# Graph attention on one core: the last output pair and the single tile turned by VectorE, adds of x and scatters two products later

## The chip, the cores and the metric

One core of one Trainium2 chip. The time is that of one execution on the device in microseconds, lower is better: a median of a few runs, and beside it one profiled execution, which every row of the trace comes from. The engines are TensorE (PE, with its weight loads as PEld), VectorE (DVE), ScalarE (ACT), GpSimd (POOL) and SyncE (SP). DMAs are issued by SP, ACT and POOL, each on a queue of its own.

## The reference

```python
h = jnp.maximum(_layernorm(x, axis=-1), 0.0)           # x: 2708 x 1024, float32
q = h @ W_q.T + b_q
k = h @ W_k.T + b_k
v = h @ W_v.T + b_v
z = (q @ k.T) / sqrt(1024)
z = z * adj                                            # adj: 0 or 1, density 0.0014771
z = jnp.where(z == 0.0, -10000.0, z)
out = x + relu(softmax(z, axis=1) @ v)
```

A row of adj has about four ones. The rest of its row of scores is -10000 and vanishes in the softmax, so a row of the output needs a handful of rows of h and no more.

## The kernel before

The keys' projection is folded into that of the queries (M, formed in the first hundred microseconds), and the values' projection is applied after the sum: a row of the output is relu(u @ W_v + b_v) + x, where u is the weighted sum of the neighbours' rows of h. Rows are sorted by their number of neighbours, so that a tile of 128 sorted rows needs K gathers of 128 rows each. `tab` holds, for each sorted row, its neighbours and its number in x.

Of the sorted tiles, 20 form ten q pairs (units 0 to 9) and 20 form ten o pairs (units 10 to 19); the last o pair is (16, 9), and tile 8 is left alone (`single`). A unit is one product of a 256x1024 block with a 1024x1024 matrix, done by `multiply` as seven smaller products of a 2x2 scheme (Strassen's in Winograd's form), each of four matmuls of 128x512 on one PSUM bank. Its operands a11, a12, a22 and s1 to s4 are formed one unit ahead by `blocks`: `upper` takes both halves of the first tile, `lower` those of the second, and VectorE forms s1 to s4. `between` starts the first two products of the next unit ahead of the last one of this unit, and for tile 8 the first product of the single.

A tile has to be turned for this (its columns on the partitions). There are two ways:

- on PE: `half_turned` issues four transposes of 128x128 into PSUM, and ScalarE copies them out (line 718) or VectorE adds from them. `turned` does both halves of a tile.
- "faced": ScalarE copies the finished sum u into v with its columns rearranged (line 944), stores v to `u_dram` (line 946), SP loads it back by quarters with `by_quarters` (line 700, four DMAs of 128 KB into a tile named or), and `faces` has VectorE transpose blocks of 32x32 (line 705).

`sums` decides which way a tile goes (line 940), by the place (unit and step) at which its sum is complete. `near` keeps a sum in SBUF (`held`) when its unit is close.

The attention runs beside the products as a generator (`attention`: `scores` multiplies gathered rows with q rows, L863; `weights`; `sums`, L923). `advance(share)` lets it run so many estimated microseconds of VectorE at each of the seven steps `after(0)` to `after(6)` of a unit. VectorE's order is the written one; for PE, ScalarE, POOL and SP a scheduler orders the instructions from unit 4 on. All four then run in their fixed order.

The result of an o unit is written into two y tiles (a pool of four buffers); `add_x` gathers rows of x onto it with an adding DMA, and `scatter` writes it to its rows of the output, both from POOL (lines 1109 and 808). `send` places a scatter behind the add of the next tile. For the last pair `ends` gathers the rows of x first and VectorE adds. `tail` handles the last 20 rows.

Of the kernel before, what the change touches and what calls it, by code (L numbers as in the profile page):

```python
# [18 lines left out]
P = 128  # L19
# [46 lines left out]
def tile_preln_masked_attention(  # L66
# [852 lines left out]
    def sums(t):  # L919
        u, coef, m = us.pop(t)  # L920
        for s in range(0 if t in EMPTY else 1, K[t]):
            fill()
            chained(lambda: nc.vector.scalar_tensor_tensor(  # L923
                u, g_of[t][s], coef[:, s:s + 1], u, op0=ALU.mult, op1=ALU.add))
            free.append(g_of[t][s])
            yield 1.3
        fill()
        if t in HOSTS:
            chained(lambda: nc.vector.scalar_tensor_tensor(
                u[:HP], g_of[t][K[t]][:HP], m[:HP, 3:4], u[:HP], op0=ALU.mult, op1=ALU.add))  # L930
            free.append(g_of[t][K[t]])
            yield 1.3
            fill()
        g_of.pop(t)
        if t == SECOND:
            nc.sync.dma_start(v_dram, u)
            whole_second.append(True)
            return
        unit = next((n for n, pair in enumerate(units) if pair[0] == "o" and t in pair[1:]), len(units))
        if now < [unit - 2, 2] and unit <= len(q_pairs) + 4:  # L940
            faced_tiles.add(t)
        if t in faced_tiles:
            v = row_tile(f"v_{t}")
            nc.scalar.copy(v.rearrange("p (a c r) -> p c a r", a=QUADS, r=QP),
                           u.rearrange("p (c a r) -> p c a r", a=QUADS, r=QP))
            nc.scalar.dma_start(u_dram[t * P:(t + 1) * P, :], v)
        elif near(t):
            held[t] = u
        else:
            nc.sync.dma_start(u_dram[t * P:(t + 1) * P, :], u)  # L950
        done.add(t)
# [159 lines left out]
    def o_results(ta, tb):  # L1111
        ya = work.tile([P, D], FT, tag="q", name=f"y_{ta}", bufs=4)
        yb = work.tile([P, D], FT, tag="q", name=f"y_{tb}", bufs=4)
        if (ta, tb) == o_pairs[-1]:
            return ends(ya, ta, yb, tb)

        def c11(X):
            nc.scalar.activation(ya[:, lo], X, AF.Relu)

        def c22(Y, p5):  # L1120
            nc.vector.tensor_add(p5, copied(Y), p5)
            nc.scalar.activation(yb[:, hi], p5, AF.Relu)

        def c12(Z, u2):
            nc.vector.tensor_add(u2, Z, u2)
            nc.scalar.activation(ya[:, hi], u2, AF.Relu)
            if ta == NT - 2:

                nc.sync.dma_start(tail_dram, ya[P - 1:, :])
            send(add_x(ya, ta))  # L1130
            sent.append((ya, ta))

        def c21(Y):
            nc.scalar.activation(yb[:, lo], Y, AF.Relu)  # L1134
            send(add_x(yb, tb))
            sent.append((yb, tb))

        return c11, c22, c12, c21

# [23 lines left out]

        return c11, c22, c12, c21

    sent = []

    def send(behind):

        while sent:  # L1170
            y, t = sent.pop(0)
            with tc.issue_after(behind.ins):
                scatter(y, t, P)

    def tail(t):
        n = tiles[t][1]
        y = work.tile([P, D], FT, tag="q", name=f"y_{t}", bufs=4)
        nc.sync.dma_start(y[:n], tail_dram.to_broadcast([n, D]))
        add_x(y, t, n)
        scatter(y, t, n)  # L1180

    def of_wv(i, j):

# [41 lines left out]
    for n, unit in enumerate(units):  # L1225
# [4 lines left out]
            ordered.enter_context(tc.manual_schedule(engines={mybir.EngineType.DVE}))  # L1230
            nc.sync.dma_start(bp_dram, bp_sb[0:1, :])
        turn = n in (0, FIRST - 1)
        share = 20.9 / 7
        nxt = units[n + 1] if n + 1 < len(units) else None
        if nxt is not None and nxt[0] == "o":
            share -= 2.3 / 7 * len(set(nxt[1:]) & faced_tiles)
# [1 line left out]

        def after(i):
            now[1] = i  # L1240
            if (n, i) in steps_ahead:
                follow(steps_ahead[n, i])
            if (n, i) == (2, 5):
                owe(8)
                owe(9)
                rows_of[FIRST] = load_rows(units[FIRST])
                owe(10)
                owe(6)
                owe(7)
                rows_of[FIRST + 1] = load_rows(units[FIRST + 1])  # L1250
                pooled.close()
            if (n, i) == (FIRST, 1):
                for g in slots[:HIGH - 3]:
                    nc.vector.memset(g, 0.0)
            b11, b12, b21, b22 = M[:, 0, 0], M[:, 0, 1], M[:, 1, 0], M[:, 1, 1]
            for at, place, src in (((-1, 0), b12, of_wv(0, 1)), ((0, 0), b11, of_wv(0, 0)), ((0, 2), T[:, 1], of_wv(1, 1)),
                                   ((0, 3), b21, of_wv(1, 0)), ((0, 4), b22, of_wv(1, 1))):
                if (n - last_q, i) == at:
                    nc.sync.dma_start(place, src)
            for at, place, a, b in (((0, 2), T[:, 0], b12, b11), ((0, 4), T[:, 1], T[:, 1], T[:, 0]),  # L1260
                                    ((1, 0), T[:, 2], b22, b12), ((1, 1), T[:, 3], b21, T[:, 1])):
                if (n - last_q, i) == at:
                    nc.vector.tensor_sub(place, a, b)
            if (n - last_q, i) == (1, 1):
                free.extend(M.rearrange("p i j (a c) w -> p i j a (c w)", a=2)[:, 0, 1, a, :] for a in range(2))
            if (n, i) == (FIRST, 5):
                next(stream)
            if (n, i) == (FIRST, 6):
                chain.append(behind[-1])
                next(stream)  # L1270
                nc.vector.tensor_tensor(bad, bad, total, op=ALU.not_equal)
            if (n, i) == (FIRST + 1, 6):
                marked(EARLY, NT)
            if (n, i) == (FIRST + 2, 4):
                nc.vector.tensor_scalar(msq, msq, MLIMIT, None, op0=ALU.is_gt)
            if n > FIRST + 1 or n == FIRST + 1 and i > 1:
                advance(share)
            if nxt is not None:

                if i == (3 if n == 0 else 4 if turn else 0):  # L1280
                    ops_of[n + 1] = blocks(*rows_of[n + 1], nc.gpsimd if n + 1 < FIRST - 1 else None)
                    with tc.issue_after(products[-1].ins) if n + 1 == FIRST else nullcontext():
                        ops_of[n + 1][1]()
                if i == (4 if n == 0 else 5 if turn else 2):
                    ops_of[n + 1][2]()
                    rows_of.pop(n + 1)
                    if n == last_q - 1:
                        all_rows()
                if i == 3:
                    banks_of[n + 1] = banks_for(bp_sb)  # L1290
                if i == 6 and n + 2 < FIRST:
                    natural_rows(n + 2)
                if i == (2 if n in (FIRST, last_q) else 4) and n + 2 > FIRST and n + 2 < len(units) and n + 2 not in rows_of:
                    while units[n + 2][0] == "o" and not done.issuperset(units[n + 2][1:]):
                        advance(1.0)
                    rows_of[n + 2] = load_rows(units[n + 2])
            if (n, i) in steps_at:
                follow(steps_at[n, i])
            if (n, i) == (3, 4):
                searched()  # L1300
            if (n, i) == (3, 5):
                for s in range(8, HIGH):
                    for c in range(0, D, D // 4):
                        clear = nc.gpsimd.memset(slots[s][:, c:c + D // 4], 0.0)
                        tc.add_manual_dep(clear.ins, counted_at[-1].ins.name,
                                          mybir.DependencyInfo(mybir.DependencyClass.Sync, mybir.DependencyReason.DATA),
                                          reason="not beside the counts")
            if i == 3 and units[n - 1][0] == "o" and NT - 2 in units[n - 1][1:]:
                tail(NT - 1)
            if nxt is None and i == 1:  # L1310
                while alone not in done:
                    advance(1.0)
                r, = load_rows(("o", alone))
                single["turned"] = turned(r, "alone")
            if nxt is None and i == 3:
                single["banks"] = banks_for(bp_sb)
            if n == last_q - 1 and i == 4:

                nc.sync.dma_start(bp_sb, bv.to_broadcast([P, D]))
            if (n, i) == (last_q, 1):  # L1320
                nc.vector.tensor_sub(bp_sb[:, NB:], bp_sb[:, NB:], bp_sb[:, :NB])
# [233 lines left out]
```

## Time and profile before

| | |
|---|---|
| median of three runs | 639.91 us (639.73 to 640.34) |
| the profiled execution | 639.94 us, its span 638.1 us |
| granted PE clock | 0.997 |
| PE busy | 98% of the span |
| VectorE busy | 82% |
| ScalarE, GpSimd busy | 44%, 56% |
| HBM | 292 GB/s over the span |

A row of a timeline gives start, length, engine, line of the kernel, operation, output and inputs with their shapes, and in brackets how long the engine had been idle and what ended that. "u", "or", "pt" and so on are the names of tiles without their numbers. A matmul of float32 shows as two records. The tail behind the last product is part of the span.

### The profile page before, as it was taken

The numbers are of one execution on the slowest core, as the hardware profiler recorded it, in microseconds if no ns is written. First come the engines' busy times: TensorE is split into PE (matmuls) and PEld (weight loads), VectorE is DVE, ScalarE is ACT, GpSimd is POOL, SyncE is SP. The second block draws the span as 40 slices with busy tenths as digits, with TensorE's granted clock in tenths as the row PEclk, the third lists the DMA queues.
The fourth block names the chain that finished last, engine by engine and source line by source line (L and its number), as shares of the span: only waits on it lengthen the run. The fifth ranks groups of instructions, "written<-read, shape, count | busy, mean of one in ns | idle before, by whom it ended". The sixth has DMA issues, their size and how long they took to land.

```text
span 638.1 us, 6156 instructions
## 1 busy us (share of the span) xinstructions
PE 627.8 (98%) x1651; PEld 317.9 (50%) x1651; DVE 522.4 (82%) x1016; ACT 283.6 (44%) x423; POOL 360.2 (56%) x383
## 2 busy tenths in 40 slices
PE   9999999999999999999999999999999999999994
PEld 5777766444444444444444444444444444444441
DVE  5999888997997625999888999999999889989121
ACT  3538985849667533424342144343342432333200
POOL 2639960885768357565651663476466878633311
PEclk9999999999999999999999999999999999999998
DMA  8999997598796439996798998999999999853631
GB/s 335 407 362 321 342 351 286 200 323 330 255 379 231 171 95 317 327 323 223 233 299 289 290 414 222 295 344 311 363 382 325 325 290 291 266 145 77 187 119 50
DMA packets 60192, 176.96 MB, mean 277 GB/s; under 512 B 9799, under 2 KB 15255, under 8 KB 59512
## 3 DMA queue, kind: packets, MB, share of 16 engines
q0 software_dynamic: 25136, 78.41, 39.4%
q1 hardware_dynamic: 29514, 78.61, 35.0%
q10 hardware_dynamic: 5502, 19.48, 7.8%
q8 instruction: 15, 0.25, 0.2%
q14 instruction: 25, 0.20, 0.1%
HBM read 145.65 MB, written 40.74 MB: 292 GB/s over the span
## 4 chain that ended last, share of the span: by engine, by line
PE 90%; issue 4%; POOL 2%; DMA 2%; DVE 1%; POOLq 0%; ACT 0%; ACTq 0%; DVEq 0%
PE ps L1010 40%; PE psy L1010 29%; PE ps_y L476 6%; PE ps_x L476 4%; PE ps_z L476 4%; PE pt L415 4%; POOL g L610 2%; DMA v_dram<-u 1%; DMA M<-h_dram,tab 1%; PE ps_y L511 1%; DVE junk L863 0%; PE ps_h L1218 0%; PE ps_v L594 0%; DVE u L923 0%; DVE s L722 0%
## 5 line engine op out<-in xcount | busy, mean ns | idle before, releaser
L610 POOL DMA_INDIRECT g<-h_dram,tab x94 | 120.2, 1278 | 79.9 <-DVE u L923 30.0
L1010 PE MATMUL psy<-wlow,s 128*128 128x512 f32 x320 | 144.0, 592 | 0.0
L1010 PE MATMUL ps<-M,a 128*128 128x512 f32 x320 | 144.0, 593 | 0.0
L863 DVE SCALAR_TENSOR_TENSOR junk<-g,pq 128x1024 uint8<-128x1024 f32 x93 | 113.8, 1224 | 13.4 <-DMA g<-h_dram,tab 10.4
L1010 PEld LDWEIGHTS ps<-M,a 128*128 128x128 f32 x320 | 59.7, 190 | 70.4 <-issue 69.1
L923 DVE SCALAR_TENSOR_TENSOR u<-g,coef,u 128x1024 f32<-128x1024 f32 x69 | 88.4, 1281 | 7.0 <-ACT u L912 5.8
L1010 PEld LDWEIGHTS psy<-wlow,s 128*128 128x128 f32 x320 | 59.6, 190 | 69.2 <-issue 69.0
L389 DVE FIND_INDEX8 at<-ones,adj 128x8 uint32<-128x685 f32 (+1 forms) x88 | 74.5, 864 | 0.0
L1010 PE MATMUL ps<-wlow,s 128*128 128x512 f32 x160 | 72.0, 593 | 0.4 <-DVE s L722 0.4
L1010 PE MATMUL ps<-M,s 128*128 128x512 f32 x160 | 72.1, 592 | 0.0
L1010 PE MATMUL psy<-wlow,a 128*128 128x512 f32 x160 | 72.0, 593 | 0.0
L368 ACT ACTIVATE sized<-adj 128x2708 uint8<-128x2708 f32 (+1 forms) x22 | 54.3, 2467 | 7.4 <-DMA adj<-in_adj_dram 6.1
L298 POOL TENSOR_TENSOR hsum<-hsum,x 128x256 f32<-128x256 f32 (+1 forms) x56 | 38.6, 732 | 26.2 <-DVE wlow L444 22.5
L1109 POOL DMA_INDIRECT y<-in_x_dram,tab x19 | 34.2, 1798 | 28.9 <-ACT y L1134 12.1
L1010 PEld LDWEIGHTS ps<-wlow,s 128*128 128x128 f32 x160 | 30.3, 190 | 38.9 <-issue 38.5
L1010 PEld LDWEIGHTS psy<-wlow,a 128*128 128x128 f32 x160 | 30.3, 190 | 38.5 <-issue 37.3
L1010 PEld LDWEIGHTS ps<-M,s 128*128 128x128 f32 x160 | 30.3, 190 | 38.1 <-issue 37.4
L808 POOL DMA_INDIRECT out_dram<-y,tab x21 | 27.4, 1306 | 32.0 <-DMA y<-in_x_dram,tab 15.8
L912 ACT ACTIVATE u<-g,coef 128x1024 f32<-128x1024 f32 x18 | 20.7, 1149 | 35.8 <-DVE coef L911 35.6
L276 ACT ACTIVATE x<-x,r 128x1024 f32<-128x1024 f32 (+1 forms) x22 | 25.9, 1232 | 6.6 <-POOL r L266 6.6
L722 DVE TENSOR_TENSOR s<-a,pt 128x512 f32<-128x512 f32 x30 | 19.2, 681 | 10.9 <-ACT a L718 10.9
L476 PE MATMUL ps_y<-wlow 128*128 128x512 f32 x64 | 27.6, 592 | 0.0
(251 smaller groups left out, 843.3 us busy)
## 6 DMA issues: line engine op xcount, KB each, us to landing
adj<-in_adj_dram SPq DMA_DIRECT2D x21, 1354.0 KB, 11.5
x<-in_x_dram SPq DMA_DIRECT2D x21, 512.0 KB, 8.2
h_dram<-x ACTq DMA_DIRECT2D x21, 512.0 KB, 7.4
q_late<-q SPq DMA_DIRECT2D x12, 512.0 KB, 5.1
pq<-q_late SPq DMA_DIRECT2D x12, 512.0 KB, 6.6
u_dram<-v ACTq DMA_DIRECT2D x10, 512.0 KB, 6.4
or<-u_dram SPq DMA_DIRECT2D x40, 128.0 KB, 7.0
M<-in_wv_dram SPq DMA_DIRECT2D x4, 1024.0 KB, 8.4
```

Of the source, the lines that this page charges most:

```text
L276: nc.scalar.activation(xs[i][:n], xs[i][:n], AF.Relu, bias=r[:n, 4, i:i + 1], scale=r[:n, 3, i:i + 1])
L298: small.append(nc.gpsimd.tensor_add(hsum[:n, cols], hsum[:n, cols], xt[:n, cols]))
L368: nc.scalar.activation(sized[:n], a[:n, :, :PW], AF.Abs, accum_out=total[:n, t:t + 1])
L389: nc.vector.max_index(at[:n, k - first_k, g, :], ones[:n, 0:8], a[:n, g, :])
L415: nc.tensor.transpose(pt[:, c, :], xt[:, k * P:(k + 1) * P], ident)
L476: mm = nc.tensor.matmul(bank, a_tile(o + H * a[0], a[1], i), b(o), start=first and o == 0, stop=(o == H - 1), skip_group_check=True)
L610: return nc.gpsimd.indirect_dma_start(out=dst, out_offset=None, in_=src, in_offset=off, bounds_check=N - 1, oob_is_err=False)
L808: to = nc.gpsimd.indirect_dma_start(out=out, out_offset=bass.IndirectOffsetOnAxis(ap=ptab.bitcast(U32)[:n, t, SLOTS:SLOTS + 1], axis=0), i ...
L863: chained(lambda: nc.vector.scalar_tensor_tensor(junk, g_of[t][s], 1.0, tq[t], op0=ALU.mult, op1=ALU.mult, accum_out=zall[:, t, s:s + 1]))
L923: chained(lambda: nc.vector.scalar_tensor_tensor(u, g_of[t][s], coef[:, s:s + 1], u, op0=ALU.mult, op1=ALU.add))
L1010: mm = nc.tensor.matmul(bank, a[:, c, :], b[:, c, :], start=False, stop=(c == 3), skip_group_check=True)
L1109: return nc.gpsimd.indirect_dma_start(out=y[:n], out_offset=None, in_=x, in_offset=off, compute_op=ALU.add)
```

## The change

- The tiles of the last pair (16 and 9) and the single tile 8 are always faced: `or unit >= len(units) - 1`. Tile 8 is loaded at the end of the last unit but one, and turned whole by VectorE at step 1 of the last.
- The add of x for a result is no longer issued where the result is written, but two products later (`due`, `add_due`), and a scatter stays back by one more add (`stay`).
- The tail tile is taken from the pool of rows instead of the pool of y, and its scatter goes through `sent` too.
- The share of VectorE per step grows from 20.9/7 to 21.5/7 in the last five units.

```diff
-        if now < [unit - 2, 2] and unit <= len(q_pairs) + 4:
+        if now < [unit - 2, 2] and unit <= len(q_pairs) + 4 or unit >= len(units) - 1:
             faced_tiles.add(t)
...
-            send(add_x(ya, ta))
-            sent.append((ya, ta))
+            due.append((now[0], 5, ya, ta))
...
             nc.scalar.activation(yb[:, lo], Y, AF.Relu)
-            send(add_x(yb, tb))
-            sent.append((yb, tb))
+            due.append((now[0] + 1, 1, yb, tb))
...
-    sent = []
-    def send(behind):
-        while sent:
-            y, t = sent.pop(0)
+    sent, due = [], []
+    def add_due():
+        while due and due[0][:2] <= tuple(now):
+            y, t = due.pop(0)[2:]
+            send(add_x(y, t), 1)
+            sent.append((y, t, P))
+    def send(behind, stay=0):
+        while len(sent) > stay:
             with tc.issue_after(behind.ins):
-                scatter(y, t, P)
+                scatter(*sent.pop(0))
...
-        y = work.tile([P, D], FT, tag="q", name=f"y_{t}", bufs=4)
+        y = row_tile(f"y_{t}")
         nc.sync.dma_start(y[:n], tail_dram.to_broadcast([n, D]))
         add_x(y, t, n)
-        scatter(y, t, n)
+        sent.insert(0, (y, t, n))
...
-        share = 20.9 / 7
+        share = (20.9 if n < len(units) - 5 else 21.5) / 7
...
         def after(i):
             now[1] = i
+            add_due()
...
             if nxt is None and i == 1:
+                uT = work.tile([P, D], FT, tag="hT", name="T_alone", bufs=2).rearrange("p (c q) -> p c q", q=P)
+                faces(uT, single["rows"], 0, DC)
+                single["turned"] = uT
+            if n == len(units) - 2 and i == 6:
                 while alone not in done:
                     advance(1.0)
-                r, = load_rows(("o", alone))
-                single["turned"] = turned(r, "alone")
+                single["rows"], = load_rows(("o", alone))
```

In the order of the instructions this shows at three places. First PE, from the first two products of the last pair's predecessor to the last pair's own; u_16 and u_9 are the sums of tiles 16 and 9. Before:

```order
L1010 MATMUL ps1_3541<-wlow_171,s1_3520 128x512 x4
L1010 MATMUL psy_3427<-wlow_171,a22_3357 128x512 x4
L415 MATMUL pt_3598<-ident_75,u_16_3416 128x128 x4
L415 MATMUL pt_3605<-ident_75,u_16_3416 128x128 x4
L1010 MATMUL psy_3571<-wlow_171,s2_3524 128x512 x4
L415 MATMUL pt_3633<-ident_75,u_9_3499 128x128 x4
L415 MATMUL pt_3640<-ident_75,u_9_3499 128x128 x4
L1010 MATMUL ps0_3539<-M_148,a12_3464 128x512 x4
```

and after:

```order
L1011 MATMUL ps1_3544<-wlow_171,s1_3526 128x512 x4
L1011 MATMUL psy_3426<-wlow_171,a22_3360 128x512 x4
L1011 MATMUL psy_3588<-wlow_171,s2_3530 128x512 x4
L1011 MATMUL ps0_3542<-M_148,a12_3475 128x512 x4
L1011 MATMUL ps1_3544<-M_148,s4_3532 128x512 x4
```

The four rows of transposes are gone, and the two of u_8 one unit later are gone in the same way. Second VectorE at the end of the program, around the turning of tile 8, which is new there (before, ScalarE copied T_alone out of PSUM). zs and many belong to a sum that decides whether the data need the general path (not taken here), y_16 and p5 to the results of the last pair. After:

```order
L705 STREAM_TRANSPOSE T_alone_3710<-or_8_3698 128x4x8x32
L1145 SCALAR_TENSOR_TENSOR y_16_3703<-ps0_3655,y_16_3703 128x512
L1340 SCALAR_TENSOR_TENSOR zs_3753<-zall_102,keys_93 128x352
L1341 TENSOR_TENSOR zs_3753<-zall_102 128x352
L1342 SCALAR_TENSOR_TENSOR zs_3753<-zs_3753 128x352
L1343 TENSOR_REDUCE many_139<-zs_3753 128x1
L1155 TENSOR_TENSOR u2_3716<-ps1_3657,u2_3716 128x512
L1350 TENSOR_TENSOR many_139<-many_139,deg_98 128x1
L1145 SCALAR_TENSOR_TENSOR y_16_3703<-u2_3716,y_16_3703 128x512
L1352 TENSOR_TENSOR many_139<-many_139,deg_98 128x1
L1151 TENSOR_TENSOR p5_3691<-psy_3685,p5_3691 128x512
```

and before:

```order
L1343 TENSOR_TENSOR many_139<-many_139,deg_98 128x1
L1146 SCALAR_TENSOR_TENSOR y_16_3701<-ps0_3660,y_16_3701 128x512
L1156 TENSOR_TENSOR u2_3723<-ps1_3662,u2_3723 128x512
L1146 SCALAR_TENSOR_TENSOR y_16_3701<-u2_3723,y_16_3701 128x512
L1152 TENSOR_TENSOR p5_3692<-psy_3686,p5_3692 128x512
```

The zs group used to stand ahead of y_16; now it stands behind the turning, and between it and the read of bank psy by p5 there are nine steps. Third POOL, from the add of x for tile 14 on. Before:

```order
L1109 DMA y_14_3590<-in_x_dram,tab_97 128x1024
L808 DMA out_0_dram<-y_10_3447,tab_97 2708x1024
L612 DMA y_16_3701<-in_x_dram,tab_97 128x1024
L612 DMA y_9_3702<-in_x_dram,tab_97 128x1024
L1109 DMA y_1_3591<-in_x_dram,tab_97 128x1024
L808 DMA out_0_dram<-y_14_3590,tab_97 2708x1024
L808 DMA out_0_dram<-y_1_3591,tab_97 2708x1024
L612 DMA y_alone_3780<-in_x_dram,tab_97 128x1024
```

and after:

```order
L1110 DMA y_14_3605<-in_x_dram,tab_97 128x1024
L808 DMA out_0_dram<-y_15_3445,tab_97 2708x1024
L612 DMA y_16_3703<-in_x_dram,tab_97 128x1024
L808 DMA out_0_dram<-y_10_3446,tab_97 2708x1024
L808 DMA out_0_dram<-y_14_3605,tab_97 2708x1024
L1110 DMA y_1_3606<-in_x_dram,tab_97 128x1024
L612 DMA y_9_3704<-in_x_dram,tab_97 128x1024
L612 DMA y_alone_3773<-in_x_dram,tab_97 128x1024
L808 DMA out_0_dram<-y_1_3606,tab_97 2708x1024
```

Each scatter (out_0_dram) has moved behind one more add of x; the gather into y_16 stands right behind the scatter of tile 15, whose buffer it takes.

More of the change, by code (lines that the diff above doesn't have):

```diff
@@ L939, in sums @@
         unit = next((n for n, pair in enumerate(units) if pair[0] == "o" and t in pair[1:]), len(units))
-        if now < [unit - 2, 2] and unit <= len(q_pairs) + 4:
+        if now < [unit - 2, 2] and unit <= len(q_pairs) + 4 or unit >= len(units) - 1:
             faced_tiles.add(t)
+        print("done", t, "at", now, "unit", unit, t in faced_tiles)
         if t in faced_tiles:
```

## The prediction

> **What bounds the kernel now.** I read the page first, then who TensorE (PE) waited for, then the chain that ended last.
>
> ```profile
> span 638.1 us, 6156 instructions
> PE 627.8 (98%) x1651; PEld 317.9 (50%) x1651; DVE 522.4 (82%) x1016; ACT 283.6 (44%) x423; POOL 360.2 (56%) x383
> ```
> ```profile
> PE ps_y L511 <- POOL hsum L121: 1.2, 1, 1.2
> PE ps L1010 <- DVE s L722: 0.4, 1, 0.4
> ```
> PE is busy for 627.8 of 638.1 us. In the whole span it waits twice: 1.2 us at the start and 0.4 us once for VectorE. What is left, 638.1 - 627.8 - 1.6 = 8.7 us, is the tail after its last product. So each microsecond taken from PE's own work shortens the run, as long as nothing that PE reads comes later than PE does. The chain near the end shows what the change takes away:
>
> ```profile
> 571.59 0.88 PE pt L415 x8
> ...
> 575.90 0.88 PE pt L415 x8
> ...
> 597.38 0.87 PE pt L415 x8
> ...
> 629.41 0.70 DVE y_alone L1371
> ```
> The first three are the turnings of tiles 16, 9 and 8. Behind the last product there is one step on VectorE (the last row) and a scatter, which the change does not touch, so that tail stays.
>
> **Removed.** The three groups of eight transposes: 0.88 + 0.88 + 0.87 = 2.63 us of a PE that never pauses there. The measured time of this profiled run was 639.94 us (span and 1.84 around it), 0.03 above the median of 639.91, so the two can be used alike. The floor is 639.94 - 2.63 = 637.31 us. ScalarE also loses five copies out of PSUM; it is busy for 44% of the span, so that is worth nothing by itself.
>
> **Added: a round trip for three tiles.** Each finished sum u is now copied on ScalarE into v, stored to DRAM, loaded back by quarters on SP's queue, and turned on VectorE. For 16 and 9 this ends long before PE needs it. For tile 8, the last, it is close, and that is the whole question. The rows for it, of VectorE and then of ScalarE (start and length in us, engine, line, operation; in brackets the idle time ahead of it and what ended that):
>
> ```profile
> 446.58 1.30 DVE L705 STREAM_TRANSPOSE a<-or 128x512 f32<-128x512 f32 x2
> 408.92 0.71 DVE L705 STREAM_TRANSPOSE a<-or 128x512 f32<-128x512 f32 x1
> 412.99 1.28 DVE L923 SCALAR_TENSOR_TENSOR u<-g,coef,u 128x1024 f32<-128x1024 f32 x1
> 547.51 1.28 DVE L923 SCALAR_TENSOR_TENSOR u<-M,coef,u 128x1024 f32<-128x1024 f32 x1
> 558.72 2.60 DVE L923 SCALAR_TENSOR_TENSOR u<-g,coef,u 128x1024 f32<-128x1024 f32 x2
> 562.38 0.69 DVE L1121 TENSOR_TENSOR p<-taken,p 128x512 f32<-128x512 f32 x1
> 571.74 0.08 DVE L863 DVE_READ_ACCUMULATOR junk<-g,pq 128x1 f32 x1
> 574.59 5.25 DVE L923 SCALAR_TENSOR_TENSOR u<-g,coef,u 128x1024 f32<-128x1024 f32 x4 [1.66 <-ACT u L912]
> 579.75 1.28 DVE L722 TENSOR_TENSOR s<-a,pt 128x512 f32<-128x512 f32 x2
> 582.27 2.60 DVE L923 SCALAR_TENSOR_TENSOR u<-M,coef,u 128x1024 f32<-128x1024 f32 x2
> 586.70 1.28 DVE L929 SCALAR_TENSOR_TENSOR u<-g,m,u 64x1024 f32<-64x1024 f32 x1
> 589.49 0.52 DVE L1331 SCALAR_TENSOR_TENSOR zs<-zall,keys 128x352 f32<-128x352 f32 x1
> ```
> ```profile
> 419.21 1.05 ACT L944 COPY v<-u 128x1024 f32<-128x1024 f32 x1 [0.57 <-DVE u L923]
> 420.29 0.33 ACTq L946 DMA_DIRECT2D u_dram<-v  x1
> 549.38 1.15 ACT L912 ACTIVATE u<-M,coef 128x1024 f32<-128x1024 f32 x1 [1.48 <-DVE coef L911]
> 561.33 0.58 ACT L1075 COPY taken<-psy 128x512 f32<-128x512 f32 x1 [1.85 <-PE psy L1010]
> ```
> *When is u_8 complete?* Before, at 586.70 + 1.28 = 587.98. Both engines work in a fixed order, so each step put ahead delays it:
> - the copy v_16 stands ahead of the first multiple of tile 9 on ScalarE: u_16 is complete at 548.79, the copy ends at 549.84 where that multiple had begun at 549.38: +0.5;
> - the copy v_9 and its store stand ahead of the copy "taken": 561.32 + 0.5 + 1.05 + 0.33 + 0.58 = 563.8, where the add behind it on VectorE would have begun at 562.38 + 0.5: +0.9;
> - two turnings for tile 16: +1.3. For tile 9, two turnings with the four adds behind them took 412.99 - 408.92 = 4.07; the four adds alone, between the rows at 579.75 and 582.27, take 2.52: +1.55;
> - the add of p that stood behind the last sum now stands ahead of it: +0.6;
> - the wait of 1.66 for ScalarE shrinks, since ScalarE has no copies from PSUM ahead of that multiple, and the short wait before it is filled by the turnings: I take -0.7.
>
> Together +4.15: u_8 is complete at 592.1, its copy at 593.2.
>
> *When must T_alone be there?* PE reads it first, and the product right behind is added on a bank that VectorE must have read:
>
> ```profile
> 590.35 3.60 PE L1010 MATMUL ps<-wlow,s 128*128 128x512 f32 x8
> 611.82 3.60 PE L1010 MATMUL ps<-M,T_alone 128*128 128x512 f32 x8
> 615.25 3.60 PE L1010 MATMUL psy<-wlow,a 128*128 128x512 f32 x8
> ```
> PE reaches T_alone at 611.82 - 2.63 = 609.2 and that product at 612.6. But on VectorE, T_alone now stands ahead of everything up to the read of that bank: four operations of the size of the row of 0.69, four of 0.52 and two tiny ones, 5.0 us. So the turning has to end by 612.6 - 5.0 = 607.6, earlier than the 609.2 that PE's own read would allow.
>
> *The trip between.* Store and quarter loads have rows of their own; the first answer is for v, the others for the quarter loads of three stretches (380 to 395, 395 to 405 and 431 to 440 us), and last the stretches as a whole (their last two numbers are the share of DMA time and GB/s):
>
> ```profile
> DMA to landing us min/median/max: 6.1/6.4/6.9
> ```
> ```profile
> L700 SPq DMA_DIRECT2D or<-u_dram x8: 302/394/432, 387.4 to 392.1; - x8
> ...
> DMA to landing us min/median/max: 4.3/5.0/5.5
> ```
> ```profile
> DMA to landing us min/median/max: 8.1/8.4/8.6
> ```
> ```profile
> DMA to landing us min/median/max: 13.1/14.1/15.1
> ```
> ```profile
> 387.00:397.00 10.00, 9.64 (x23) 4.08 (x22) 9.83 (x15) 3.89 (x7) 3.99 (x3) 1.00 0.91 191
> 401.00:412.00 11.00, 11.00 (x27) 4.90 (x26) 10.76 (x21) 4.63 (x8) 5.31 (x5) 1.00 1.06 277
> 600.00:610.00 10.00, 10.00 (x24) 4.37 (x23) 2.00 (x3) 1.17 (x2) 2.93 (x3) 1.00 0.76 209
> ```
> The store lands at 593.2 + 6.4 = 599.6. Four issues of 0.39 follow; the last goes out at about 601.0 and lands L later; the turning takes 1.3. T_alone ends at 602.35 + L, and the loss is S = L - 5.25 where that is positive. L is the term that the trace of before bounds only from afar: 4.3 to 15.1. I take the row of 380 to 395 (5.0; in all 191 GB/s with eight loads), because the stretch 600 to 610 moved 209 GB/s without quarter loads, only four are added, and nothing else stands on SP's queue; the row of 8.4 comes from a stretch with 277 GB/s and gathers every 1.3 us. L from 4.3 to 5.5 gives S from 0 to 0.3; I take 0.1. Sum: 637.31 + 0.1 = **637.4 us**.
>
> Rule against row: the Trainium skill ("DMA: Bandwidth & Descriptors", Anatomy of one DMA) puts a transfer at some 2.0 us plus its bytes at 436 GB/s. An estimate from that page is 2.3 us for a quarter and 3.2 for the store, which would leave S at 0 and the time at 637.31. The rows above disagree: 4.3 is the fastest of that stretch and 6.1 the fastest store.
>
> *Tiles 16 and 9.* The store of v_16 goes out at 551.1, lands at 557.5, its last quarter leaves at about 559.0, and VectorE comes to it at 571.74 + 0.5 + 0.9, 573.2: L up to 14 is hidden. For v_9: out at 562.9, landed 569.3, last quarter 570.8, VectorE at 580.5 (the first sum of tile 8 at 574.59 + 0.5 + 0.9 + 1.3 - 0.7 = 576.6, and three sums of 1.29): L up to 9.7 is hidden. The sums s1 are then ready at 582.6, PE wants them at 590.35 - 1.76 = 588.6.
>
> **Moved, at no cost that I can find.** On POOL's queue each scatter now stands behind one more add of x, and two gathers come ahead of an add that they stood behind. What the old order cost POOL between 410 and 600 us, then the rows of a scatter, of the last gather of h rows, of ScalarE's write into a y buffer, and of a scatter's landing:
>
> ```profile
> POOL out_dram L808 <- DMA y<-in_x_dram,tab: 7.0, 3, 3.2
> ```
> ```profile
> 550.54 1.03 POOL L808 DMA_INDIRECT out_dram<-y,tab  x1 [0.30 <-issue]
> ...
> 556.73 1.01 POOL L610 DMA_INDIRECT g<-h_dram,tab  x1 [0.30 <-issue]
> ```
> ```profile
> 563.10 0.63 ACT L1122 ACTIVATE y<-p 128x512 f32<-128x512 f32 x1 [1.19 <-DVE p L1121]
> ```
> ```profile
> out_dram<-y,tab POOLq DMA_INDIRECT x21, 6.5
> ```
> 7.0 us of POOL waiting goes, worth 0 to at most the 0.4 us that PE waited for VectorE at all, and that was near 389 us, ahead of the first scatter: I take 0. The price would be a y buffer that comes free later: tile 12's scatter leaves at about 550.5 instead of 537, lands 6.5 later at 557, and ScalarE writes the buffer again at 563.10. Six microseconds cover it. The larger budget for the last five units puts one sum (1.28) ahead of the four adds; those are 588.6 - 582.6 = 6 us early at the worst place. The tail tile in another pool and the changed place of its load on SP delay nothing that PE reads.
>
> **Rivals.**
> - *The loads of tile 8 share the DMA engines with the delayed scatters* (those of tiles 10 and 14 now stand behind tile 15's scatter and behind a gather into its buffer, so they fall into the same stretch). For it: the 8.4 row. Then S = 3.15 and 640.5: the gain is used up. From L = 6.5 on (S = 1.25) it is no longer a gain of 0.2%. Chance 0.18 for L between 6.5 and 9.1.
> - *Slower: the same loads wait as the worst did*, 13.1 to 15.1 (the stretch from 431 us). Then S = 7.9 to 9.9 and 645.2 to 647.2. It decides from L = 9.1 (S = 3.9). Against it: in that stretch gathers were queued; the last of them goes out at 556.73. With tile 9's loads beyond 9.7, which push the same step, chance 0.13.
> - *VectorE becomes the bound.* The Trainium skill ("VectorE: DVE Perf Modes", Rules for kernel authors) advises TensorE for turning 128x128. By the rows, eight blocks take 0.88 us on PE and 1.3 on VectorE, so the rule holds engine by engine, but PE is the one that is full. It would decide if the adds for the last pair came 6 us later than worked out; a further 4 us beyond that, and 639.94 - 2.63 + 4 = 641.3. Chance 0.03.
>
> **Chances and range.** Forecast with S below 1.3: 0.66. A measurement of this kernel can tell about 0.2%, 1.28 us, from no change, so faster is below 638.63 and slower above 641.19: faster 0.66, same 0.18, slower 0.16. The range goes down to 636.8 (the floor, less the 0.4 us wait should it vanish, less 0.1) and up to 640.6, which takes in S = 3.3, the row of 8.4.
>
> **What would show it.** Right: no pt rows of 571 to 598 us; the last quarter load of or_8 lands by 606.3, T_alone is turned by 607.6, PE's waits in the last 30 us are under 0.3 us, and the span is 2.5 us shorter. Wrong: a wait of PE at T_alone or at the product after it, with VectorE idle for or_8 ahead of it; a landing of or_8 over 6.5; VectorE waiting for or_16 or or_9; or ScalarE held up by a y buffer.

## The result, and the profile after

| | before | changed |
|---|---|---|
| median | 640.34 us (639.63 to 642.51, 7 runs) | 637.2 us (636.89 to 639.33, 7 runs) |
| ratio | | 0.9961, 95% interval 0.9945 to 0.9976 |
| PE busy in the profiled execution | 627.8 us | 625.4 us |

The change is faster by 0.4%, some 2.5 us of 640 (1.5 to 3.5). The ratio, which comes with the interval, is what is used below; it is not the quotient of the two medians, which would be 0.9951. The profiled execution of the changed kernel was one of its slower ones (639.16 us, span 637.1), so its span must not be set against the 638.1 of before. Its page and the list of whom PE waited for:

```profile
span 637.1 us, 6134 instructions
...
PE 625.4 (98%) x1627; PEld 315.4 (49%) x1627; DVE 524.7 (82%) x1021; ACT 284.8 (45%) x421; POOL 362.7 (57%) x383
```
```profile
PE ps_y L511 <- POOL hsum L121: 1.2, 1, 1.2
PE pt L415 <- DMA qr<-h_dram,tab: 0.7, 1, 0.7
PE ps L1011 <- DVE s L722: 0.6, 1, 0.6
PE ps_in L678 <- DVE sort L666: 0.4, 1, 0.4
```
PE has 2.4 us less to do. It waits 2.9 us in all where it waited 1.6 before, and all four waits lie in the first 391 us, ahead of everything that the change touches. These 1.3 us more of early waiting are why this one execution is only 1.0 us shorter in span. No wait of PE ends behind 391 us.

The rows that answer to those of the prediction, of VectorE, ScalarE and PE (the changed file's lines are one higher here):

```profile
573.63 1.30 DVE L705 STREAM_TRANSPOSE a<-or 128x512 f32<-128x512 f32 x2
...
580.73 0.70 DVE L705 STREAM_TRANSPOSE a<-or 128x512 f32<-128x512 f32 x1
...
591.09 1.27 DVE L929 SCALAR_TENSOR_TENSOR u<-g,m,u 64x1024 f32<-64x1024 f32 x1
604.96 1.25 DVE L705 STREAM_TRANSPOSE T_alone<-or 128x1024 f32<-128x1024 f32 x1 [11.53 <-DMA or<-u_dram]
611.04 0.69 DVE L1151 TENSOR_TENSOR p<-psy,p 128x512 f32<-128x512 f32 x1 [0.89 <-PE psy L1011]
```
```profile
562.22 1.04 ACT L945 COPY v<-u 128x1024 f32<-128x1024 f32 x1 [0.56 <-DVE u L923]
...
592.39 1.05 ACT L945 COPY v<-u 128x1024 f32<-128x1024 f32 x1 [0.56 <-DVE u L929]
593.47 0.33 ACTq L947 DMA_DIRECT2D u_dram<-v  x1
```
```profile
610.84 3.60 PE L1011 MATMUL ps<-M,T_alone 128*128 128x512 f32 x8
614.27 3.60 PE L1011 MATMUL psy<-wlow,a 128*128 128x512 f32 x8
```
The turnings of 16 and 9 have no bracket: VectorE did not wait for their rows. For tile 8 it waited 11.53 us with nothing else to do, turned at 604.96, and its add into p ended at 611.73, after 0.89 us of waiting for PE. The product that must follow that add begins at 614.27. So VectorE could have been 614.27 - 611.73 + 0.89 = 3.4 us later before PE lost anything. I call this the *room* below.

The quarter loads of tiles 16, 9 and 8, by stretch:

```profile
L700 SPq DMA_DIRECT2D or<-u_dram x4: 330/500/1092, 556.6 to 558.0; - x4
...
DMA to landing us min/median/max: 10.4/10.4/10.4
```
```profile
L700 SPq DMA_DIRECT2D or<-u_dram x4: 303/431/505, 571.0 to 572.4; - x4
...
DMA to landing us min/median/max: 3.5/3.5/3.5
```
```profile
L700 SPq DMA_DIRECT2D or<-u_dram x4: 303/430/431, 597.6 to 598.9; - x4
...
DMA to landing us min/median/max: 5.1/5.1/5.1
```
In each of these stretches the view tells the landing of one quarter of the four, which is why its three figures are equal. The same instruction landed in 10.4, 3.5 and 5.1 us. The quarter of the 5.1 is not the last one: from the last issue for tile 8, at 598.9, to the turning at 604.96 there are 6.1 us.

### The profile page after: what moved, and what is told of

It reads as the page before. It is cut to its first block, busy times and chain, and to the rows that moved or that the text cites. A ratio compares the mean times of both kernels' runs of the same rounds, so it can differ in the third digit from the quotient of the medians.

```text
span 637.1 us, 6134 instructions
## 1 busy us (share of the span) xinstructions
PE 625.4 (98%) x1627; PEld 315.4 (49%) x1627; DVE 524.7 (82%) x1021; ACT 284.8 (45%) x421; POOL 362.7 (57%) x383
## 4 chain that ended last, share of the span: by engine, by line
PE 87%; issue 4%; DVE 4%; DMA 2%; POOL 2%; POOLq 0%; ACT 0%; ACTq 0%; DVEq 0%
PE ps L1011 39%; PE psy L1011 27%; PE ps_y L476 6%; PE ps_z L476 4%; PE ps_x L476 4%; PE pt L415 4%; POOL g L610 2%; DMA v_dram<-u 1%; DVE g L1260 1%; DMA M<-h_dram,tab 1%; PE ps_y L511 1%; DVE s L722 0%; DVE at L389 0%; DVE junk L863 0%; PE ps_h L1223 0%
## 5 line engine op out<-in xcount | busy, mean ns | idle before, releaser
L610 POOL DMA_INDIRECT g<-h_dram,tab x94 | 123.7, 1316 | 81.7 <-DVE u L923 33.0
L1110 POOL DMA_INDIRECT y<-in_x_dram,tab x19 | 32.6, 1717 | 29.9 <-ACT y L1127 15.3
L808 POOL DMA_INDIRECT out_dram<-y,tab x21 | 25.7, 1224 | 17.7 <-DVE flag L1355 7.3
L760 ACT COPY ps<-bp_sb 128x512 f32<-128x512 f32 x42 | 24.6, 595 | 6.0 <-DVE y L1145 5.5
```

The lines of the kernel that those rows point to most:

```text
L610: return nc.gpsimd.indirect_dma_start(out=dst, out_offset=None, in_=src, in_offset=off, bounds_check=N - 1, oob_is_err=False)
L808: to = nc.gpsimd.indirect_dma_start(out=out, out_offset=bass.IndirectOffsetOnAxis(ap=ptab.bitcast(U32)[:n, t, SLOTS:SLOTS + 1], axis=0), i ...
L1110: return nc.gpsimd.indirect_dma_start(out=y[:n], out_offset=None, in_=x, in_offset=off, compute_op=ALU.add)
```

## The experiments

The kernel before was timed again in each of the four sets. Its median was 640.17 us in the first (the parts apart) and 640.44 in the third (how late the scatters must be, more tiles), but 647.5 in the second (which part, the room) and 645.9 in the fourth (the flags), where most executions had a granted clock of 0.987 to 0.995. The first and the fourth set ran on the same chip, the second and the third on two others, so the chip alone does not make this difference. Only ratios are compared across sets. "The deferral" below takes in the tail's new tile and the place of its scatter; no run tests that part by itself.

### The parts apart

The theory from the trace: facing three tiles is worth 2.63 us of PE, and the deferral is worth nothing.

*Facing alone*: the condition and the early load of T_alone, with adds, scatters, tail and share as before.

```diff
-        if now < [unit - 2, 2] and unit <= len(q_pairs) + 4:
+        if now < [unit - 2, 2] and unit <= len(q_pairs) + 4 or unit >= len(units) - 1:
```


> Tiles 16, 9 and 8 turned by VectorE, but adds, scatters, tail tile and shares as before. If the gain is PE's transposes alone (theory A): 2.6 us under before, as the changed kernel, ratio 0.996; PE's busy time 2.6 less. If the later adds and scatters carry part of it (theory B, at least 1 us): at most 1.6 under before. If the scatters that now lie earlier clear the DMA engines for the loads of tile 8 or crowd them, T_alone ends elsewhere than 606.2, which costs only if it ends over 3.4 us later.

Measured: 641.12 us (637.17 to 643.29, 12 runs), ratio 1.0013 (0.9996 to 1.003). No gain, with executions 6 us apart where those of before were 3.4 apart.

*Deferral alone*: `due`, `stay`, the tail tile and the share, without the facing.

> Adds of x and scatters two products later, tail tile in the pool of rows, larger share at the end; tiles 16, 9 and 8 turned on PE as before. Theory A: no change, 0 within 0.4 us of before (0.4 is what PE waited for VectorE). Theory B: 1 us or more under before. In both, POOL's waits for landed adds (7.0 us in three waits between 410 and 600 us before) fall to nearly 0.

Measured: 640.52 us (639.74 to 641.46, 11 runs), ratio 1.0009 (1.0000 to 1.0018). Nothing, as predicted. GpSimd's waits for landed adds between 410 and 600 us fell from 7.0 to 3.1 us, not to nearly nothing.

*The pair only*: the changed kernel with tile 8 turned by PE again.

```diff
-... or unit >= len(units) - 1:
+... or unit == len(units) - 1:
```


> The changed kernel, but tile 8 turned on PE as before (no round trip for it). Theory A: 0.88 + 0.88 = 1.76 us under before and 0.87 over the changed kernel. If the round trip of tile 8 costs a wait of its own, this one is as fast as the changed kernel or faster.

Measured: 638.45 us (638.06 to 639.42, 11 runs), ratio 0.9972 (0.9963 to 0.9982). PE's only turning behind 555 us in its profile:

```profile
595.50 1.04 PE L415 MATMUL pt<-ident,u 128*128 128x128 f32 x8
```
Two of three groups are gone and 1.8 us with them (2 times 0.88 = 1.76).

*The changed kernel again*, in the same set:

> The changed kernel again, without its printing while it is built, to stand beside the others on one chip. Theory A: 2.6 us under before, ratio 0.996, PE busy 625.2, no wait of PE behind 590 us. The profile of the changed kernel showed 1.3 us of waits of PE in the first 390 us that before did not have, all ahead of what the change touches; by theory A they are chance and absent or different here.

Measured: 637.73 us (636.89 to 638.99, 5 runs), ratio 0.9961 (0.9949 to 0.9974). PE is busy for 625.6 us, and its waits are others than in the first profile of this kernel: 1.2 us at the start and 1.5 us that end at 370 us, none behind.

What follows: together the parts bring 2.5 us, the facing alone nothing, the deferral (with the share) alone nothing. The theory that the rest of the change is idle ballast falls. Without it the facing's gain does not arrive.

### Which part the facing needs

Two rivals: the share (it places VectorE's side steps) or the deferral (it frees GpSimd and the DMA engines).

*Facing and the new share*:

```diff
-        share = 20.9 / 7
+        share = (20.9 if n < len(units) - 5 else 21.5) / 7
```


> Only the facing of tiles 16, 9 and 8 and the early loads of T_alone, as in the run with the facing alone (which measured no gain, 641.1 us with runs from 637.2 to 643.3), plus the new share of VectorE's side steps (21.5/7 in place of 20.9/7 in the last units). Adds of x, scatters and the tail stay as before. Theory A (facing is worth 2.6 us and any arrangement keeps it unless VectorE reaches the rows too early; the facing alone lost it because its side steps stand too early, with less than 2 us between the landing of tile 16's quarters at 569.8 and VectorE's turn at 571.7): the share pushes or leaves the side steps so that the quarters are in time, 637.5 to 638.5 and a narrow spread. Theory B (the early adds and scatters take DMA engines from the loads, and only their deferral cures that): as the facing alone, 640 to 642 with a wide spread.

Measured: ratio 0.9993 (0.9965 to 1.0021; 646.02 us against 647.5). No cure.

*Facing and the deferral, old share*:

> The changed kernel with the old share (20.9/7 everywhere): facing, deferred adds and scatters, tail's new tile, but not the new share. Theory A (the share decides): 640 to 642 with a spread of several us, as the facing alone. Theory B (the deferral is what the facing needs, since it empties the queues while the quarters load): 637.5 to 638.3, as the changed kernel, with runs within 2 us of each other.

Measured: ratio 0.9961 (0.9929 to 0.9994; 644.67 us). The whole gain, though its executions were not within 2 us of each other as expected (639.2 to 649.04): neither were those of before in this set. So the share is not needed. That the deferral is needed rests on the first set, where the facing alone (0.9996 to 1.003) and the changed kernel (0.9949 to 0.9974) are clear of each other; in this set the intervals with the deferral (0.9929 to 0.9994) and without it (0.9965 to 1.0021) overlap.

*A second profile of the facing alone*:

> The kernel with the facing alone once more, for a second profile of it, since its first one fell on one of its quick executions (638.45 us of 637.2 to 643.3). If this profile is of one above 640.5: theory A expects VectorE to wait for the rows of tile 16, 9 or 8 (the idle time ahead of a turning ends with a DMA of or or of u_dram, 2 us or more) and TensorE behind it at s1 or T_alone; theory B in its other form (the y tiles come free late, and ScalarE or VectorE wait for one) expects the wait at a y tile or at taken instead. If the waits of TensorE stand in the first 400 us, the loss has nothing to do with the facing.

It took 644.26 us. In this set that is not a long execution, since the kernel before had a median of 647.5; so it is not the kind of execution that was sought. PE and VectorE at the end:

```profile
614.94 3.70 PE L1010 MATMUL ps<-M,T_alone 128*128 128x512 f32 x8
619.42 3.70 PE L1010 MATMUL psy<-wlow,a 128*128 128x512 f32 x8 [0.79 <-DVE p L1152]
```
```profile
577.62 1.30 DVE L705 STREAM_TRANSPOSE a<-or 128x512 f32<-128x512 f32 x2 [0.90 <-DMA or<-u_dram]
...
586.00 0.71 DVE L705 STREAM_TRANSPOSE a<-or 128x512 f32<-128x512 f32 x1 [1.03 <-DMA or<-u_dram]
613.64 1.25 DVE L705 STREAM_TRANSPOSE T_alone<-or 128x1024 f32<-128x1024 f32 x1 [13.68 <-DMA or<-u_dram]
```
VectorE now waits for the rows of 16 (0.90), of 9 (1.03; 2 or more were expected) and of 8, and PE waits 0.79 us for the add that stands behind T_alone's turning. (The waits for 16 and 9 are not a mark of the facing alone: with the deferral and the old share VectorE waited 0.73 us for the rows of 9, and PE did not wait.) The room is gone. T_alone ends at 614.89, 16.0 us behind u_8 (598.89); in the changed kernel it was 13.85 (592.36 to 606.21). The facing with the new share shows the same wait of PE, at 0.3 us. So the wait that the prediction feared does appear, at the place it named. But 6.1 of the 6.9 us that PE waits in this execution stand in the first 400 us. The longest of them (3.8 us, VectorE's add of q, at 372 us) is also in the profile of the next kernel (3.9 us), which keeps its gain, so it does not come from the facing.

The first profile of the facing alone, of an execution of 638.45 us, has no wait of PE behind 391 us, but its room is smaller than the changed kernel's. Its add into p and the product that must follow:

```profile
611.38 0.68 DVE L1152 TENSOR_TENSOR p<-psy,p 128x512 f32<-128x512 f32 x1
```
```profile
613.45 3.60 PE L1010 MATMUL psy<-wlow,a 128*128 128x512 f32 x8
```
The add ends at 612.06 and did not wait for PE, so the room is 613.45 - 612.06 = 1.4 us. In the same way it is 3.4 and 3.1 us in the two profiles of the changed kernel and 2.8 us with the old share, and where PE waits (the facing alone again, the facing with the new share) there is none. With the same three tiles faced, each profile with the deferral has more room than each without it.

### How much room there is

*T_alone turned three times over*, in the changed kernel:

```diff
-                faces(uT, single["rows"], 0, DC)
+                for again in range(3):
+                    faces(uT, single["rows"], 0, DC)
```


> The changed kernel with the turning of T_alone done three times over, so that VectorE is through with it 2.5 us later (some more for side steps between). By the prediction's deadline (T_alone's end by 607.6, the rest of VectorE's work behind it 5.0 us): at 606.2 + 2.5 = 608.7 or more it would cost 1 to 2 us. By the profile of the changed kernel, where TensorE reaches T_alone's product at 610.84, VectorE's add into p5 ends 611.73 and the product that must follow it begins at 614.27: there are 2.5 us of room, and the time stays as it is, within 0.5 us.

Measured: ratio 0.9962 (0.9936 to 0.9988), the gain unchanged.

```profile
617.37 1.23 DVE L705 STREAM_TRANSPOSE T_alone<-or 128x1024 f32<-128x1024 f32 x1
621.15 0.68 DVE L1150 TENSOR_TENSOR p<-psy,p 128x512 f32<-128x512 f32 x1
```
```profile
623.04 3.60 PE L1010 MATMUL psy<-wlow,a 128*128 128x512 f32 x8
```
The last of the three turnings begins 617.37 - 614.24 = 3.1 us behind the first, and 623.04 - 621.83 = 1.2 us of room are left. Over 3 us of delay on tile 8's path made PE wait nowhere at the end. The interval of the time is 0.5% wide, so by the time alone a loss of 1 us could not be seen.

### Is it the scatter or the add that must be late

The deferral does two things in the program. It issues the adds two products later, and it lets a scatter stay back by one more add. Here only the second is kept (with the tail's part and the new share):

```diff
-            due.append((now[0], 5, ya, ta))
+            send(add_x(ya, ta), 1)
+            sent.append((ya, ta, P))
...
-            due.append((now[0] + 1, 1, yb, tb))
+            send(add_x(yb, tb), 1)
+            sent.append((yb, tb, P))
```


> The changed kernel, but the adds of x stand where they stood before the change, right behind the ReLUs of their rows; only the scatters are one add later, so that GpSimd does not reach a scatter while the add into the same rows is still landing. Theory B1 (the facing needs GpSimd's queue free: with the facing alone GpSimd stood 17.5 to 20.7 us behind 400 us before scatters that waited for an add's landing, with the deferral 4.0 to 7.8 us, and the gathers of the last tiles stand behind them): this cures it, ratio 0.996, and that wait is below 8 us. Theory B2 (it is the adds' own traffic and their wait for ScalarE's ReLU, so the adds themselves must come two products later): ratio 0.998 to 1.001, with runs as far apart as with the facing alone.

Measured: 637.58 us (637.03 to 638.94, 6 runs), ratio 0.9957 (0.994 to 0.9974). What GpSimd waited for ahead of a scatter, from 400 to 600 us, in the kernel before, in the facing alone, in the changed kernel and in this one:

```profile
POOL out_dram L808 <- DMA y<-in_x_dram,tab: 12.2, 4, 5.3
```
```profile
POOL out_dram L808 <- DMA y<-in_x_dram,tab: 12.1, 4, 4.8
```
```profile
POOL out_dram L808 <- DMA y<-in_x_dram,tab: 2.7, 1, 2.7
```
```profile
POOL out_dram L808 <- DMA y<-in_x_dram,tab: 2.8, 1, 2.8
```
So this kernel keeps the gain, with the program's adds back at their old places and only the scatters late. That does not show that the adds may stay where they were. The scheduler sets GpSimd's order, and in the trace that order of adds, scatters and gathers is the changed kernel's, from the adds near 398 us to the scatter near 597: the edit hardly moved anything. Nor had the change itself moved the adds much. Taken in order, the 19 adds that GpSimd issues from 396 us on start within 3.4 us of their times before, where two products are 6.9 us. Since the share is not needed, what sets the kernels that keep the gain apart from the facing alone is where the scatters stand and the tail's part, and these two were not taken apart. The room here is 612.62 - 610.19 = 2.4 us, against 1.4 in the first profile of the facing alone, where PE waits nearly as long in all (1.8 us, here 2.0).

Where a scatter comes one add sooner, GpSimd stands before it until an add of x has landed, some 12 us in all; the kernel before shows the same wait, and it cost nothing there. That VectorE's lateness comes from the gathers queued behind is argued from the order of the queue. The rows only point that way: VectorE's waits for gathered rows between 400 and 612 us come to 3.3, 4.0 and 5.2 us in the three profiles of the facing without the deferral, and to 2.3, 0.4, 1.5 and 3.8 us in four with it (the changed kernel twice, this one, the old share).

### More tiles

*Tiles 14 and 1 too* (`unit >= len(units) - 2`):

> The changed kernel with tiles 14 and 1 of the pair before turned by VectorE too. TensorE loses two more groups of transposes, 2 times 0.88 = 1.76 us; VectorE gains four half turnings, 2.6 us, and ScalarE two copies of 1.04 us, all ahead of u_8. If the room at the end holds (VectorE could be 3.4 us later by the profile of the changed kernel, and 2.5 us were had for nothing when T_alone was turned three times): TensorE's products come 1.76 earlier and VectorE 2.6 later, together 4.4 us against 3.4 us of room: 1 us is lost again, about 636.5 us on the first chip, ratio 0.9948. If VectorE reaches the rows of 14 or 1 before they have landed, or holds up s1: no gain over the change, 0.996 or worse.

Measured: 637.79 us (637.13 to 640.17, 11 runs), ratio 0.9958 (0.9945 to 0.9972). PE busy falls to 623.9 us and a new wait takes it back:

```profile
PE ps L1010 <- DVE T_alone L705: 1.6, 1, 1.6
```
*Tile 14 only*:

> The changed kernel with tile 14 alone of the pair before turned by VectorE too: TensorE 0.88 us less, VectorE 1.3 us and ScalarE 1.04 us more; together 2.2 us of the 3.4 us of room at the end, so the gain stays: 0.88 us below the changed kernel, ratio 0.9947. The rival: the store and loads of tile 14 (1 MB more on the queues at 535 to 550 us, where the engines of the DMA are full) delay gathers and VectorE, no gain, 0.996 or worse.

Measured: 637.37 us (635.98 to 638.17, 6 runs), ratio 0.9944 (0.9926 to 0.9962). VectorE behind T_alone, and the product that waits:

```profile
607.37 1.25 DVE L705 STREAM_TRANSPOSE T_alone<-or 128x1024 f32<-128x1024 f32 x1 [11.00 <-DMA or<-u_dram]
...
609.11 0.50 DVE L1339 SCALAR_TENSOR_TENSOR zs<-zall,keys 128x352 f32<-128x352 f32 x1
...
610.64 0.52 DVE L1342 TENSOR_REDUCE many<-zs 128x1 f32<-128x352 f32 x1
...
612.48 0.68 DVE L1150 TENSOR_TENSOR p<-psy,p 128x512 f32<-128x512 f32 x1
```
```profile
613.21 3.70 PE L1010 MATMUL psy<-wlow,a 128*128 128x512 f32 x8 [0.85 <-DVE p L1150]
```
The ratio is as expected, the reason is not: 2.2 of 3.4 us of room were to be used and PE was not to wait. The room is used up by one tile more. Four steps on `zs` (2.06 us) stand between the turning and the add, while VectorE idled 11.00 us just before. *These four steps put ahead of the turning*:

> The kernel with tile 14 turned by VectorE too, and the four long steps of the flags (on zall, 0.50, 0.51, 0.53 and 0.52 us, 2.06 in all) put ahead of T_alone's turning, into the 11.0 us in which VectorE waits for the rows, in place of behind it. In the run with tile 14 alone these four stood between T_alone and the add into p5, and TensorE waited 0.85 us for that add. If that chain is what takes part of the gain: the add ends 2.06 us earlier, the 0.85 us wait is gone with 1.2 us to spare, and the time is up to 0.85 us below the run with tile 14, some 636.5 us, ratio 0.993. If TensorE does not wait there in most executions, or the landing sets T_alone later: no difference, 0.9944.

Measured: ratio 0.9951 (0.9919 to 0.9982; 643.79 us against 645.9). The rows behind T_alone:

```profile
611.89 1.25 DVE L705 STREAM_TRANSPOSE T_alone<-or 128x1024 f32<-128x1024 f32 x1 [8.56 <-DMA or<-u_dram]
616.29 0.69 DVE L1150 TENSOR_TENSOR p<-psy,p 128x512 f32<-128x512 f32 x1 [1.25 <-PE psy L1010]
```
From the turning's end to the end of the add it now takes 2.6 us (without the wait for PE) where it took 4.5: the chain was shortened as expected. But PE also comes to T_alone's product 2.9 us later behind the turning than in the profile before, and with the old chain of 4.5 us it would not have waited in this execution either. So this profile does not show that the new order removes a wait, and the interval, 0.6% wide, cannot tell whether it is worth anything in time. None of the three is shown to beat the changed kernel. Their intervals overlap with its own.

## Why the prediction was right, point by point

- *The floor.* Foretold 2.63 us of PE; PE's busy time fell by 2.4, and the median by 3.1 between the seven runs of each, 2.5 by the ratio. Right. Tile 8's own part came out as 638.45 - 637.73 = 0.7 us, 0.88 foretold, though the intervals of these two kernels overlap.
- *u_8 complete at 592.1, its copy at 593.2.* Measured 592.36 and 593.44. The two turnings took 1.30 as priced. The agreement of the six terms together is helped by the early waits of this execution. In the profile with the scatters alone late, where PE keeps to the foretold times (612.62 for the 612.6 of the deadline), u_8 is complete at 590.86, 1.2 us sooner than the sum has it.
- *The trip.* Two terms were off, in opposite directions. The store was put at 6.4 us, and the quarter loads went out 4.2 us after the copy's end. The last of them left at 598.9 where 601.0 was foretold; from there to VectorE's start took 6.1 us where L of 5.0 was foretold. Net, T_alone ended at 606.21 where 602.35 + 5.0 = 607.35 was foretold. That the two errors cancelled is luck: with the store as priced, an L of 6.1 makes S = 0.85, and the rival of the shared engines begins at 6.5. The rule that the prediction set beside its rows is stated in that section of the Trainium skill for DMAs issued by GpSimd; here ScalarE issues the store and SyncE the loads.
- *The deadline.* From T_alone's end to the end of the add it took 611.73 - 606.21 - 0.89 = 4.6 us, 5.0 foretold. PE came to that product 1.65 us later in the profiled execution than foretold, of which 1.3 are its early waits. Where PE was on the foretold time (the scatters alone late) VectorE came sooner too, and the room was 2.4 us. So S is 0 where 0.1 was taken.
- *Tiles 16 and 9.* "L up to 14 is hidden", "up to 9.7": the landings were 10.4 and 3.5, and VectorE waited for neither. Reached at 573.63 and 580.73; foretold 573.2 and 580.5. Tile 16 was nearer to its bound than the choice of 5.0 for L suggests.
- *"Moved, at no cost that I can find", worth 0.* Right as a sum and wrong as a reading. Alone the deferral is worth 0 (1.0009). But the step "7.0 us of POOL waiting goes, worth 0 to at most the 0.4 us that PE waited" priced it against the old schedule, in which VectorE had room to be late. (Of the 7.0 us 2.7 stayed.) In the new one the room without the deferral is 1.4 us or none, and the whole gain is missing (1.0013 against 0.9961). I had costed each part with the other part absent. That the time came out right all the same is because the change has both parts in it; the prediction gives no reason why they belong together.
- *The rival of loads that share with the delayed scatters.* It went the other way: the gain is missing where the scatters are not delayed. In the stretches 590 to 600 and 600 to 610 us of the changed kernel the share of DMA time was indeed 0.74 and then 0.99:

```profile
590.00:600.00 10.00, 10.00 (x24) 4.37 (x23) 3.36 (x12) 4.02 (x6) 4.56 (x5) 1.00 0.74 194
600.00:610.00 10.00, 10.00 (x25) 4.39 (x24) 4.97 (x9) 1.18 (x2) 4.60 (x5) 1.00 0.99 316
```
  With that, the last load took 6.1 us to VectorE's start, 0.4 below where the rival begins.
- *VectorE as the bound.* Not in the change, but one tile further: with 14 faced PE waits for VectorE's add, with 14 and 1 for T_alone itself. By the Trainium skill ("VectorE: DVE Perf Modes", Rules for kernel authors) 128x128 blocks should be turned on TensorE where PSUM will do as the destination. Here PE's 0.88 us for eight blocks against 1.25 to 1.30 on VectorE agrees with the order of the two, and yet moving three tiles gained 2.5 us, since PE was the full engine; two more tiles showed no further gain.
- *What would show it.* PE turns none of the three tiles, the rows of tile 8 had landed by 604.96 and T_alone was turned by 606.21, and PE did not wait in the last 30 us: these signs held. The span was to be 2.5 us shorter and was 1.0 in the one profiled execution, for the early waits told above.

What stays open: the facing alone lost its whole 2.6 us by the medians, but its second profile shows 0.79 us of waiting at the end, and its first, of an execution of 638.45 us, none. Both are among the shorter executions of their sets. In neither does a wait appear that explains an execution of 643 us in the first set. That the deferral is needed is shown by the times, and that it gives room by the profiles; how a loss of 2.6 us comes about without it is not shown. Nor is it shown what the tail's part does by itself.

## What to carry to other kernels

When a chain of work is moved off a full engine onto one with slack, count the slack at the place where the full engine next reads, and count it again for every queue that feeds the receiving engine: here a wait on GpSimd that cost nothing before went with the loss of the whole gain after. Judge the parts of a change together as well as one by one, since a part that is worth nothing alone can be what the other rests on. To measure slack, add a known delay: repeat a step and read in the trace whether the full engine waits, since the time alone may be too coarse to tell. And when an edit moves instructions that a scheduler orders, look in the trace whether they moved.

## What was not expected of the hardware

The same 128 KB quarter load landed in 3.5 us at 572 us and in 10.4 us at 557 of one execution, and the 512 KB store ahead of tile 8's loads was out in at most 4.2 us where another stretch had 6.1 to 6.9. And one and the same kernel, that of before, had a median of 640.2 us in one set and 647.5 in another, on another chip, but also 645.9 in a later set on the first chip; the profiles of the second set show a wait of PE near 375 us of up to 3.9 us and granted clocks down to 0.993 where the first had 0.996.
